# Four GNN layers in one kernel: layer 0's first layer norms in pairs, and the row sums of the adjacency matrix shared by VectorE and POOL

## The chip, the cores and the metric

The kernel runs on one core of a Trainium2 chip. The metric is the device time of one execution in microseconds (us). The core has five engines that work side by side and wait for each other through semaphores: TensorE (PE in the profile, with its weight loads as PEld), VectorE (DVE), ScalarE (ACT), GpSimd (POOL) and SyncE (SP), which here only issues DMA transfers. An engine runs its own instructions strictly in the order in which they were recorded.

## The reference

There are 4096 nodes with 64 features each, and one dense 4096 x 4096 float32 adjacency matrix `adj` (64 MiB), which all four layers use. Each layer computes `x = x + layer(relu(layernorm(x)), adj)`. Cut to what matters here:

```python
# layer 0                       h = adj @ h;  x += relu(h @ W.T + b)
# layer 1                       h = lorentz(h, W); q = lorentz(h, Wq); k = lorentz(h, Wk)
att = adj * sigmoid((2 + 2 * (qm @ k.T)) / att_scale + att_bias)
support = att @ h             # then each row is divided by its Lorentz norm
# layer 2
deg = jnp.maximum(adj.sum(axis=1, keepdims=True), 1e-08)
w = adj / deg
log_ij = _logmap(x[:, None, :], x[None, :, :], c)
agg = jnp.einsum('ij,ijc->ic', w, log_ij)
# layer 3                       ranks of the non-zero entries of each row, then w @ support
```

The row sums `deg` are needed in layer 2 alone. Since the matrix passes through the core in every layer anyway, the kernel makes them while it is there for layers 0 and 1.

## The kernel before, in words

**Tiling.** The 4096 rows are eight row blocks `ib` of 512 rows. For each block the transposed matrix comes in 16 groups `g`; a group is one tile `adj` of 128 partitions x 2 x 512 floats (512 KB), issued by `feed` on SP's queue, in a fixed order. Ten buffers hold such tiles in layers 0 and 1 (a pool of six and one of four). A buffer is free again when all readers of its tile are done (`used` counts them for the planner); SP's next issue into it waits for that.

**Layer 0.** `before0(ib)` makes the layer norm of 512 rows into `HA`: two reductions and two element-wise steps on VectorE, a square on ScalarE, and the power -0.5 on POOL (`power`, a tensor_tensor with `ALU.pow`). It is called once for each of the eight blocks. `l0_sums` adds each `adj` tile times `HA` into a PSUM accumulator `acc`; group `g` needs the rows of block `g // 2`, so already the first block of sums needs all eight layer norms. When the last group of a block is in, `after0` (ScalarE copies `acc` to `e`, PE multiplies by `W0T`, VectorE adds to `x`) and then `before1` (layer norm, two Lorentz linears, transposes to `qT` and `kT`) follow.

**Layer 1.** For each pair of tiles: `l1_atts` (PE, `mm<-qT,kT`), `l1_sigmoids` (ScalarE), `l1_weights` (VectorE, `sig<-sig,adj`), `l1_sums` (PE, `acc<-sig,HL`); after the last of a block `after1`, and `before2` for layer 2. Blocks 0 and 1 run together at first, with groups 14 and 15 kept for later, since these need the last block of `kT`.

**Row sums.** `degree_sums(layer, work)` adds tiles on VectorE into a buffer `dg` (128 x 2 x 512): the first by a copy, each further one by a tensor_tensor. Blocks 0 and 7 add all 16 tiles in layer 0; blocks 1 to 6 add 12 in layer 0 and the four of `LEFT` in layer 1. `after0` and `after1` add the two halves of `dg`, sum over partitions on PE (`tr<-ones_f,dg`), and write or add to `deg`.

**Order.** The instructions of all stages are recorded by generators that yield an engine and a due time. `in_turn` picks the one that can start first by the planner `Pace`, whose `cost` estimates each operation's duration; so a change of a cost or of a due time can shift the order on every engine, in the later layers too. The layer norms and what follows a block stand in a queue `tail`, of which the first two entries advance at a time. Tensors in `Pace.KEPT` (among them `HA`, `x` and `RT`) carry no due time for the planner, but the recorded waits between engines are real. `constants` issues the parameter loads on ScalarE's queue from 20 us of planned time, and at 36 us records `later_constants`: patterns that layers 1 to 3 need.

**Layers 2 and 3.** Layer 2 goes by tile pairs through a chain PE, ACT (`v<-mm`), POOL (`l2_clamps`, `v<-v`), ACT, DVE, PE. When a block is complete, `after2` and `before3` follow, with two POOL powers (`r_nn` and `ln_r`). Layer 3 does not use POOL for its tiles. Every instruction passes the recording helper `InOrder`, so the profile gives one line, L129, to nearly all.

The functions that the change touches:

Of the kernel before, what the change touches and what calls it, by code (L numbers as in the profile page):

```python
# [18 lines left out]
P = 128  # L19
# [5 lines left out]
CB = W // P  # L25
G = 2
NG = NC // G
LEFT = (3, 7, 11, 15)
EARLY = 12
BEHIND = NG - CB // G  # L30
LATE = BEHIND - CB // G
# [27 lines left out]
class Pace:  # L59
# [16 lines left out]
    def cost(self, engine, op, out, ins, rest, kw):  # L76
        n = per_partition(out)
        if engine == "PE":

            w, x = ins[0], ins[1]  # L80
            shape = [32 if k <= 32 else 64 if k <= 64 else 128 for k in (w.shape[0], per_partition(w))]
            change = 0.0 if shape == self.shape else 0.11
            self.shape = shape
            if op == "transpose":
                return change + 0.14
            share = 1 if n < 128 else min(128 * 128 // math.prod(shape), 4)
            passes = 4 if x.dtype == F32 else 1
            return change + max(passes * n / 2400 + 0.06, 0.27 if passes == 4 else 0.06) / share
        if engine == "ACT":
            if any(arg is AF.Sigmoid for arg in rest):  # L90
                n += n // 6
            return 0.18 + n / 1200 + (0.19 if "accum_out" in kw else 0.0)
        if engine == "POOL":
            return 1.65 if ALU.pow in kw.values() or n <= 8 else 0.25 + n / 300
        many = [ap for ap in ins if per_partition(ap) > 1]
        big = max([n] + [per_partition(ap) for ap in ins])
        psum = any(self.name(ap).split("_")[0] in ("mm", "acc", "tr") for ap in ins)
        return 0.12 + big / (1920 if len(many) <= 1 and not psum and op != "tensor_reduce" else 960)
# [38 lines left out]
def kernel(ctx: ExitStack, tc: tile.TileContext, a: dict, out: bass.AP):  # L137
# [111 lines left out]
    def later_constants():  # L249


        ACT.activation(es, scal[:, 0:3], AF.Exp)

        DVE.reciprocal(att_a, scal[:, 4:5])
        DVE.tensor_scalar(att_a, att_a, 2.0, None, ALU.mult)
        DVE.tensor_add(att_b, att_a, scal[:, 3:4])
        for t, one in [(t, 1.0) for t in rbs] + [(t, 0.25) for t in lbs]:
            POOL.memset(t, 0.0)
            for k in (1, 3):
                POOL.memset(t[:, :, k, 1:2], one)  # L260


        near_f = st["rows"].tile([P, P], F32, name="near_f", bufs=1)
        make_lower_triangular(nc, near_f, val=-STEP, diag=False)
        for q in range(4):
            b = slice(q * Q, (q + 1) * Q)
            DVE.tensor_copy(far[b, :], near_f[b, b])
        diag_f = st["rows"].tile([P, P], F32, name="diag_f", bufs=1)
        DVE.tensor_scalar(diag_f, ident, STEP * MAX_NEIGH, None, ALU.mult)
        DVE.tensor_add(near_f, near_f, diag_f)  # L270
        DVE.tensor_copy(near, near_f)


        DVE.memset(pick, 0.0)
        DVE.memset(spread, 0.0)
        for k in range(KH):
            DVE.memset(pick[:, k, k : k + 1], 1.0)
        for r in range(4):
            b = slice(r * Q, (r + 1) * Q)
            for h in range(2):  # L280
                to = spread[b, h, :, h * NC // 2 : (h + 1) * NC // 2]
                DVE.tensor_copy(
                    to.rearrange("p q (k r) -> p q k r", r=4)[:, :, :, r],
                    ident[b, r * Q : r * Q + KH].unsqueeze(1).to_broadcast([Q, 4, KH]),
                )

    def cs(ib):
        return slice(ib * CB, (ib + 1) * CB)

    def ws(ib):  # L290
        return slice(ib * W, (ib + 1) * W)
# [4 lines left out]
    def rt(name, shape, dtype=F32):  # L296
        return rows.tile(shape, dtype, tag=f"{name}_{slot['now']}", name=name, bufs=1)
# [38 lines left out]
    def bank():  # L336
        k = spare.pop(0)
        t = ps_tr.tile([P, W], F32, tag=f"tr{k}", name="tr", bufs=1)
        in_use.append((t, k))
        return t  # L340
# [78 lines left out]
            )  # L419


    def before0(ib, st):
        yield from layernorm_relu(ib, st["h0"][:, cs(ib), :])

    def before1(ib, st):
        h = rt("h", [P, CB, D])
# [121 lines left out]
    def after0(ib, acc, st):  # L548
        e = rows.tile([P, W], F32, tag="e", name="e")
        ACT.copy(e, acc)  # L550
        st["acc_free"][ib % 2] = pace.latest
        yield ON_V, lambda: st["dg_done"].get((0, ib))
        dg = st["dg"][0, ib]
        DVE.tensor_add(dg[:, 0, :], dg[:, 0, :], dg[:, 1, :])
        yield TURN

        ps = bank()
        v, n = ps[:, 0 : CB * D].rearrange("p (c k) -> p c k", k=D), CB * D
        for c in range(CB):
            b = slice(c * P, (c + 1) * P)  # L560
            PE.matmul(v[:, c, :], e[:, b], W0T, start=True, stop=True)
            PE.matmul(ps[:, n + c : n + c + 1], dg[:, 0, b], ones_f, start=True, stop=True)
        st["dg_free"][ib % 2] = pace.latest
        yield ON_V
        DVE.tensor_copy(deg[:, cs(ib), :], ps[:, n : n + CB].unsqueeze(2))
        s = rt("h", [P, CB, D])
        DVE.tensor_add(s, v, b0.to_broadcast([P, CB, D]))
        DVE.scalar_tensor_tensor(
            x[:, cs(ib), :], s, 0.0, x[:, cs(ib), :], ALU.max, ALU.add
        )  # L570
        yield ON_V

    def after1(ib, acc, st):
        e = rows.tile([P, W], F32, tag="e", name="e")
        ACT.copy(e, acc)
        st["acc_free"][ib % 2] = pace.latest
        yield ON_V, lambda: st["dg_done"].get((1, ib)) if (1, ib) in st["dg"] else 0.0
        dg = st["dg"].get((1, ib))
        if dg is not None:
            DVE.tensor_add(dg[:, 0, :], dg[:, 0, :], dg[:, 1, :])  # L580
        yield TURN
        ps = bank()
        v, n = ps[:, 0 : CB * D].rearrange("p (c k) -> p c k", k=D), CB * D
        for c in range(CB):
            b = slice(c * P, (c + 1) * P)
            PE.matmul(v[:, c, :], e[:, b], twice, start=True, stop=True)
            if dg is not None:
                PE.matmul(ps[:, n + c : n + c + 1], dg[:, 0, b], ones_f, start=True, stop=True)
        if dg is not None:
            st["dg_free"][ib % 2] = pace.latest  # L590
        yield ON_S
        s = rt("h", [P, CB, D])
        ACT.copy(s, v)
        sq = rt("r_sq", [P, CB, D])
        ACT.activation(sq, v, AF.Square)
        if dg is not None:
            new = rt("r_c", [P, CB, 1])
            ACT.copy(new, ps[:, n : n + CB].unsqueeze(2))
        yield ON_V
        if dg is not None:  # L600
            DVE.tensor_add(deg[:, cs(ib), :], deg[:, cs(ib), :], new)
        n = rt("r_n", [P, CB, 1])
        DVE.tensor_reduce(n, sq[:, :, 1:D], AX.X, ALU.add)
        DVE.tensor_sub(n, n, sq[:, :, 0:1])
# [106 lines left out]
    def latest(*times):  # L711
        return None if None in times else max(times)

    def in_turn(threads):
# [31 lines left out]

    st = {
        "h0": HA[:, :, 0:D],
        "dg": {}, "dg_done": {}, "acc_free": [0.0, 0.0], "dg_free": [0.0, 0.0],
    }  # L750
    rows_at = {}
    opened = {}
# [65 lines left out]


    def group(layer, ib, g):  # L820
        degree = (g in LEFT and 0 < ib < NB - 1) == (layer == 1)
        return {"layer": layer, "ib": ib, "g": g, "degree": degree, "left": 1 + degree, "at": 0.0}

# [25 lines left out]
            )  # L851
        return accs[k]

    def degree_sums(layer, work):

        dg = st["dg"]
        for d in work:
            if not d["degree"]:
                continue
            first = (layer, d["ib"]) not in dg  # L860
            yield "DVE", lambda: latest(
                arrival(d, 3.0), st["dg_free"][d["ib"] % 2] if first else 0.0
            )
            if first:
                t = w01.tile([P, G, W], F32, tag="dg", name="dg", bufs=2)
                dg[layer, d["ib"]] = t
                st["dg_free"][d["ib"] % 2] = None
                DVE.tensor_copy(t, d["adj"])
            else:
                t = dg[layer, d["ib"]]  # L870
                DVE.tensor_add(t, t, d["adj"])
            used(d)
            if d is [e for e in work if e["degree"] and e["ib"] == d["ib"]][-1]:
                st["dg_done"][layer, d["ib"]] = pace.latest

    for ib in range(NB):
        follow(with_mark(0, ib, before0(ib, st)))
        tail[-1]["at"] = 4.5 + 0.4 * ib

    def l0_sums():  # L880
        for d in l0:
# [10 lines left out]
    def constants():  # L892
        for k in range(len(loads) - 1):
            yield "ACT", lambda: 20.0 + 0.5 * k
            loads.pop(0)()
        loads[0]()
        yield "ACT", lambda: 36.0
        later_constants()
        loads.pop(0)

# [80 lines left out]

    def second_part():

        yield "ANY", lambda: latest(l1[-1].get("summed"), *st["dg_free"])
        early.close()
        adj_pools.pop()
        late["pool"] = ctx.enter_context(tc.tile_pool(name="late", bufs=1))
# [414 lines left out]
    def l3_sum():  # L1404
# [39 lines left out]
            (l2_coshs(), 0, once), (l2_weights2(), 1, lambda d: 2 if d["two"] else 1 if d["first"] else 0),  # L1444
        ),
        l2_clamps(), l2_gathers(), l3_weights(), l3_pass(), l3_counts(), l3_masks(),
        degree_sums(0, l0), degree_sums(1, l1), constants(),
    ])


# [43 lines left out]
```

## Time and profile before

| what | value |
|---|---|
| time, median of 3 runs | 1186.83 us (1185.45 to 1261.08) |
| profiled execution, its own time | 1186.61 us |
| span from first to last instruction in it | 1184.6 us |
| PE busy | 1078.5 us (91%) |
| DVE busy | 929.3 us (78%) |
| ACT busy | 783.1 us (66%) |
| POOL busy | 324.3 us (27%) |
| bytes moved by DMA | 271.76 MB |
| mean granted TensorE clock | 0.976 |

About 2.0 us of the profiled execution lie outside the span. Layer 0's last accumulator is copied out at 211.59 us, layer 1's last at 485.60 us, and layer 2's tile work ends near 960 us. In the view by stages each row gives the stretch, its length, the busy time of PE, PEld, DVE, ACT and POOL with the number of instructions, the granted TensorE clock, the busy share of the DMA engines and the rate in GB/s. In the timeline a row gives start, duration, engine, line, operation, tiles (`out<-in`), shapes, how many were merged, and in brackets the idle time of the engine before it and what ended it.

### The profile page before, as it was taken

To read this page: it belongs to the slowest core of one execution; us is meant where nothing else is said; L and a number is where in the kernel's file an instruction comes from. 1 tells how busy PE (TensorE), PEld (TensorE's weight loads), DVE (VectorE), ACT (ScalarE), POOL (GpSimd) and SP (SyncE) were. 2 spreads that over 40 slices of the span, in tenths; PEclk is the share of its full clock that TensorE was granted. 3 is DMA by queue.
4 is the path that set the end of the run, shared out by engine and by line. 5 is a ranking of instruction groups with operands and counts; after the bars stand their busy time and mean duration, and the time that the engine had idled before them with its cause. 6 is when DMAs were issued, how large, how long until landed. Compare 5 with 4: busy or idle time off the path is not lost.

```text
span 1184.6 us, 15638 instructions
## 1 busy us (share of the span) xinstructions
PE 1078.5 (91%) x5367; PEld 449.7 (38%) x5392; DVE 929.3 (78%) x1523; ACT 783.1 (66%) x1250; POOL 324.3 (27%) x172
## 2 busy tenths in 40 slices
PE   3899999999999999889989989999889789999997
PEld 1234444333333333244444444444344333333332
DVE  6888888869988988688888888898989985555550
ACT  1055456777767766789988778787876655555554
POOL 2222321102000010344454464464654420000000
PEclk9898999999999999899999999999998999999999
DMA  7899999865777765535434534444364389888830
GB/s 275 330 405 350 401 378 348 303 216 199 245 249 235 249 232 192 195 107 196 162 128 172 175 121 166 160 150 163 113 206 151 124 343 367 321 314 312 303 112 9
DMA packets 77191, 271.76 MB, mean 229 GB/s; under 512 B 10040, under 2 KB 11064, under 8 KB 77112
## 3 DMA queue, kind: packets, MB, share of 16 engines
q1 hardware_dynamic: 75456, 270.57, 63.7%
q8 instruction: 42, 0.69, 0.2%
q10 hardware_dynamic: 1656, 0.20, 0.1%
q14 instruction: 37, 0.30, 0.1%
HBM read 269.68 MB, written 1.05 MB: 229 GB/s over the span
## 4 chain that ended last, share of the span: by engine, by line
PE 49%; DVE 18%; ACT 11%; issue 10%; POOL 8%; DMA 3%; SPq 0%; ACTq 0%; POOLq 0%; DVEq 0%
PE acc L129 23%; PE mm L129 17%; PE tr L129 8%; DVE dg L129 5%; POOL v L129 4%; ACT wt L129 3%; DVE w L129 3%; ACT v L129 2%; DMA adj<-in_adjT_dram 2%; ACT t L129 2%; DVE t L129 2%; POOL lo_s L129 1%; DVE sig L129 1%; ACT sig L129 1%; POOL ln_r L129 1%
## 5 line engine op out<-in xcount | busy, mean ns | idle before, releaser
L129 PE MATMUL acc<-w,HA 128*65 128x256 f32 (+1 forms) x736 | 256.3, 485 | 13.0 <-DVE others L129 7.1
L129 POOL TENSOR_SCALAR v<-v 128x1024 f32<-128x1024 f32 x72 | 204.8, 2845 | 211.5 <-ACT v L129 205.4
L129 ACT ACTIVATE wt<-mm 128x1024 uint16<-128x1024 f32 x124 | 120.3, 1021 | 94.1 <-PE mm L129 94.1
L129 ACT ACTIVATE sig<-mm,att_b,att_a 128x1024 f32<-128x1024 f32 x128 | 148.3, 1202 | 40.9 <-PE mm L129 39.9
L129 DVE TENSOR_TENSOR sig<-sig,adj 128x1024 f32<-128x1024 f32 x128 | 152.5, 1221 | 25.2 <-ACT sig L129 25.0
L129 PE MATMUL acc<-adj,HA 128*64 128x512 f32 x512 | 128.4, 639 | 24.3 <-DVE HA L129 24.1
L129 DVE TENSOR_TENSOR dg<-dg,adj 128x1024 f32<-128x1024 f32 x114 | 139.2, 1221 | 2.2 <-DMA adj<-in_adjT_dram 0.6
L129 PEld LDWEIGHTS acc<-w,HA 128*65 128x65 f32 x736 | 98.1, 143 | 104.7 <-issue 56.6
L129 PE MATMUL mm<-qT,kT 64*128 64x512 f32 x512 | 129.5, 619 | 3.3 <-ACT sig L129 3.3
L129 PE MATMUL acc<-sig,HL 128*64 128x512 f32 x512 | 123.3, 604 | 1.6 <-DVE sig L129 1.5
L129 DVE SCALAR_TENSOR_TENSOR t<-mm,t 128x1024 f32<-128x1024 f32 x72 | 83.6, 1161 | 44.4 <-ACT t L129 43.9
L129 PE MATMUL acc<-wt,S 128*64 128x512 bf16 (+1 forms) x479 | 97.7, 387 | 3.5 <-issue 2.4
L129 PE MATMUL mm<-RT,LT 64*128 64x512 f32 (+1 forms) x288 | 79.7, 631 | 15.9 <-DVE t L129 15.2
L129 ACT ACTIVATE t<-t 128x1024 f32<-128x1024 f32 x72 | 72.6, 1008 | 31.9 <-DVE t L129 31.3
L129 ACT ACTIVATE v<-mm 128x1024 f32<-128x1024 f32 x72 | 69.8, 970 | 30.7 <-PE mm L129 30.6
L129 POOL TENSOR_TENSOR ln_r<-ln_v,minus_half 128x4 f32<-128x4 f32 x32 | 49.3, 1542 | 148.7 <-DVE ln_v L129 148.7
L129 DVE TENSOR_TENSOR w<-t,adj 128x1024 f32<-128x1024 f32 x72 | 84.0, 1167 | 1.5
L129 DVE SCALAR_TENSOR_TENSOR t<-t,v 128x1024 f32<-128x1024 f32 x72 | 83.7, 1163 | 1.8 <-ACT t L129 0.9
L129 ACT ACTIVATE v<-v,minus 128x1024 f32<-128x1024 f32 x72 | 78.4, 1089 | 7.8 <-POOL v L129 7.7
L129 DVE TENSOR_TENSOR w<-tr,adj 128x512 f32<-128x512 f32 x120 | 77.5, 681 | 1.1 <-PE tr L129 1.1
L129 PE MATMUL tr<-ident,t 128*128 128x128 f32 x480 | 66.1, 280 | 11.9 <-DVE t L129 8.2
L129 DVE TENSOR_SCALAR RT<-adj 128x1024 bf16<-128x1024 f32 x74 | 50.4, 698 | 33.3 <-PE mm L129 33.0
(208 smaller groups left out, 1395.6 us busy)
## 6 DMA issues: line engine op xcount, KB each, us to landing
adj<-in_adjT_dram SPq DMA_DIRECT2D x512, 512.0 KB, 4.8
x<-in_x_dram SPq DMA_DIRECT2D x4, 256.0 KB, 3.7
out_dram<-h SPq DMA_DIRECT2D x8, 128.0 KB, 2.8
b<-in_b_dram ACTq DMA_DIRECT2D x2, 32.0 KB
W<-in_W_dram ACTq DMA_DIRECT2D x3, 16.0 KB, 4.4
W0T<-in_W0T_dram ACTq DMA_DIRECT2D x2, 16.0 KB, 3.4
W1T<-in_W1T_dram ACTq DMA_DIRECT2D x1, 16.0 KB, 3.4
W1T<-in_b_dram ACTq DMA_DIRECT2D x1, 0.2 KB
```

The source lines that it names most:

```text
L129: done = self.tc.keep_in_program_order(getattr(self.engine, op)(*args, **kw))
```

## The change

Four things are edited.

1. `before0(k)` now makes the layer norm of two blocks (1024 rows) at once; it is called four times instead of eight. Its scratch lies in `HL` and `qT`, which layer 1 fills later.
2. `later_constants` is split. The three steps that layer 1 needs stay in `constants`; the patterns of POOL are due at 60 us, those of VectorE at 150 us, in five pieces.
3. The row sums: of the 16 groups of each block, VectorE adds the eight even ones in layer 0 into `dg`; POOL adds groups 3, 7, 11 and 15 in layer 0 and groups 1, 5, 9 and 13 in layer 1, straight into `RT[:, ws(ib)]` (`RT` is filled with something else by layer 2's `before2` later). VectorE adds the two halves of `dg` to the same place. The partition sum moves from `after0` to `after1`, for all eight blocks.
4. The planner's costs for POOL change: a power of n columns costs 0.5 + 0.25 n (was 1.65), other operations 0.25 + n/390 (was n/300), a memset 0.11 + n/1200.

```diff
-LEFT = (3, 7, 11, 15)
+POOL_0, POOL_1 = (3, 7, 11, 15,), (1, 5, 9, 13,)
+FRONT_0, FRONT_1 = (3, 7, 11, 15,), (1, 5, 9, 13,)
...
         if engine == "POOL":
-            return 1.65 if ALU.pow in kw.values() or n <= 8 else 0.25 + n / 300
+            if op == "memset":
+                return 0.11 + n / 1200
+            return 0.5 + 0.25 * n if ALU.pow in rest else 0.25 + n / 390
...
+        def patterns():
+            yield "POOL", lambda: 60.0
...
+        def weights_of_ranks():
+            yield "DVE", lambda: 150.0
...
-    def before0(ib, st):
-        yield from layernorm_relu(ib, st["h0"][:, cs(ib), :])
+    def before0(k, st):
+        c = slice(2 * k * CB, 2 * (k + 1) * CB)
+        xs, xc, to = x[:, c, :], st["HL"][:, c, :], st["h0"][:, c, :]
+        sq = st["qT"][:, 2 * k * W : (2 * k + 1) * W].rearrange("p (c d) -> p c d", d=D)
+        m, v, r = (rt(name, [P, 2 * CB, 1]) for name in ("lo_g", "lo_t", "lo_n"))
+        DVE.tensor_reduce(m, xs, AX.X, ALU.add)
+        DVE.scalar_tensor_tensor(xc, m.to_broadcast(xs.shape), -1.0 / D, xs, ALU.mult, ALU.add)
+        yield ON_S
+        ACT.activation(sq, xc, AF.Square)
+        yield ON_V
+        DVE.tensor_reduce(v, sq, AX.X, ALU.add)
+        DVE.tensor_scalar(v, v, 1.0 / D, LN_EPS, ALU.mult, ALU.add)
+        power(r, v, -0.5)
+        yield ON_V
+        DVE.scalar_tensor_tensor(to, xc, 0.0, r.to_broadcast(xs.shape), ALU.max, ALU.mult)
...
     def after0 (ib, acc, st):
-        yield ON_V, lambda: st["dg_done"].get((0, ib))
-        DVE.tensor_add(dg[:, 0, :], dg[:, 0, :], dg[:, 1, :])
-            PE.matmul(ps[:, n + c : n + c + 1], dg[:, 0, b], ones_f, start=True, stop=True)
-        DVE.tensor_copy(deg[:, cs(ib), :], ps[:, n : n + CB].unsqueeze(2))
+        v = yield from times(e, W0T, D, ON_V)
...
     def after1(ib, acc, st):
+        yield TURN, lambda: None if sums_left[ib] else 0.0
+            PE.matmul(
+                ps[:, n + c : n + c + 1], RT[:, (ib * CB + c) * P : (ib * CB + c + 1) * P], ones_f,
+                start=True, stop=True,
+            )
+        ACT.copy(deg[:, cs(ib), :], ps[:, n : n + CB].unsqueeze(2))
...
     def group(layer, ib, g):
-        degree = (g in LEFT and 0 < ib < NB - 1) == (layer == 1)
+        late = g in (POOL_1 if ib else FRONT_1)
+        by = "POOL" if late or g in (POOL_0 if ib else FRONT_0) else "DVE"
+        degree = by if late == (layer == 1) else None
...
+    def degree_sums():                      # VectorE's share, layer 0
+            for d in mine:
+                if d is mine[0]:
+                    DVE.tensor_copy(t, d["adj"])
+                else:
+                    DVE.tensor_add(t, t, d["adj"])
+            yield "DVE", lambda: opened.get(("sums", ib))
+            for c in range(G):
+                DVE.tensor_add(RT[:, ws(ib)], RT[:, ws(ib)], t[:, c, :])
+
+    def degree_sums_beside(work):           # POOL's share
+            to, ib = RT[:, ws(d["ib"])], d["ib"]
+            yield "POOL", lambda: arrival(d, 3.0)
+            if ("sums", ib) in opened:
+                POOL.tensor_tensor(to, to, d["adj"][:, 0, :], ALU.add)
+                yield "POOL", lambda: 0.0
+                POOL.tensor_tensor(to, to, d["adj"][:, 1, :], ALU.add)
             else:
+                POOL.tensor_tensor(to, d["adj"][:, 0, :], d["adj"][:, 1, :], ALU.add)
+                opened["sums", ib] = pace.latest
...
-    for ib in range(NB):
-        follow(with_mark(0, ib, before0(ib, st)))
-        tail[-1]["at"] = 4.5 + 0.4 * ib
+    for k in range(NB // 2):
+        follow(before0(k, st))
+        tail[-1]["at"] = 4.3 + 0.4 * k
```

## The prediction

> **What bounds the kernel now.** I read the view by stages first, then the timeline of the front, then the tile views of the operations that the change moves, last the chain of waits.
>
> ```profile
> 0.00:50.00 50.00, 25.88 (x86) 7.33 (x88) 39.15 (x86) 5.30 (x11) 13.21 (x36) 0.90 0.81 287
> 50.00:100.00 50.00, 46.61 (x236) 21.09 (x234) 43.20 (x68) 21.27 (x85) 11.53 (x6) 0.93 1.00 390
> 100.00:150.00 50.00, 47.22 (x258) 21.56 (x256) 41.45 (x68) 24.27 (x99) 14.36 (x7) 1.00 0.99 382
> 150.00:210.00 60.00, 58.50 (x304) 25.05 (x302) 52.11 (x79) 34.88 (x122) 11.89 (x7) 1.00 0.94 363
> 210.00:490.00 280.00, 270.23 (x1238) 99.00 (x1234) 232.43 (x449) 200.74 (x365) 32.98 (x20) 1.00 0.70 233
> 490.00:960.00 470.00, 425.26 (x1948) 199.75 (x1950) 409.89 (x593) 375.42 (x441) 236.03 (x93) 0.96 0.44 156
> 960.00:1185.00 225.00, 204.79 (x1306) 75.92 (x1328) 111.06 (x185) 121.25 (x131) 4.30 (x4) 1.00 0.71 260
> ```
>
> Layer 0 (to 210 us) is held by transfers: DMA share 0.94 to 1.00, PE next to full, VectorE 41 to 43 of 50 us. Layer 1 (to 490) is held by PE, 270 of 280 us, with DMA at 0.70. In layer 2 PE, DVE and ACT alternate. So a VectorE microsecond saved in layer 1 is worth little; in layer 0 what counts is the stream of tiles.
>
> Five-microsecond slices of the same view show up to 419 GB/s. At 417 a tile of 524,288 B takes 1.26 us. Against that rate the first 50 us owe 45 x 417 + 5 x 169 (first slice) less 50 x 287 = 5.3 MB, **12.6 us**; 50 to 210 owe 160 x 417 less 60.4 MB moved = 6.3 MB, **15.1 us**. The front's debt has its reason in the timeline:
>
> ```profile
> 33.05 1.01 POOL L129 TENSOR_TENSOR ln_r<-ln_v,minus_half 128x4 f32<-128x4 f32 x1 [2.11 <-DVE ln_v L129]
> ...
> 35.84 1.85 POOL L129 TENSOR_TENSOR ln_r<-ln_v,minus_half 128x4 f32<-128x4 f32 x1 [1.78 <-DVE ln_v L129]
> ...
> 37.45 1.83 DVE L129 CAST far<-near_f 32x32 bf16<-32x32 f32 x4 [0.18 <-issue]
> ...
> 40.59 1.05 DVE L129 CAST spread<-ident 32x16 bf16<-32x16 f32 x8
> 41.68 0.43 DVE L129 SCALAR_TENSOR_TENSOR HA<-ln_xc,ln_r 128x256 f32<-128x256 f32 x1
> ...
> 42.16 10.18 PE L129 MATMUL acc<-adj,HA 128*64 128x512 f32 x40 [3.42 <-DVE HA L129]
> ...
> 45.52 0.59 ACT L129 COPY e<-acc 128x512 f32<-128x512 f32 x1 [11.23 <-PE acc L129]
> ```
>
> The eighth layer norm reaches `HA` only at 41.68, behind 5 us of constants on VectorE; PE waits for it, no buffer comes free, the transfers pause. The first accumulator leaves at 45.52.
>
> **The change, term by term.**
>
> *Front.* With 1024 rows at once a reduction or step takes about 0.69 us (the 512-column rows: `dg<-dg` 0.686), a ScalarE square 0.6, the power of 8 columns 1.64 (`lo_s` with no neighbour). In the recorded order: reduce 4.36 to 5.05, centre to 5.8, square to 6.45, reduce and scale to 7.4, power to 9.1, next pair's two steps and reductions, `HA` of blocks 0 and 1 at about 11.1; the others at 14.7, 18.4 and 20.3. Now they come at 16.2 to 41.7. Tiles 5, 9 and 13, the first to need blocks 2, 4 and 6, land near 15, 20 and 25, so PE follows the arrivals and block 0 ends near 31 instead of 45.5. POOL begins its additions only after its four powers, about 19.4, which holds tiles 4 and 8; ten buffers cover that in part. I take 9 of the 12.6 us back: **-9** (bounds -12 and -4). ScalarE's parameter loads and SP's order are unchanged. The constants move to about 150 us on VectorE; there VectorE's freed time hides them. Without that cover they cost their 5 us.
>
> *VectorE and POOL in layer 0.* Now an inner block costs VectorE 0.69 + 11 x 1.22 + 0.69 + 0.16 = 15.0 us of sums and 5.3 of the rest, 20 of the 22 us that a block lasts. After: 0.69 + 7 x 1.22 + 2 x 0.69 = 10.6, with the rest 15.9. POOL gets 7 additions of 512 columns. No row has them; the nearest is `x<-x,b`, 256 columns, 0.727 us: doubled 1.45, or 1.35 with the slope of the `v<-v` rows (2.77 at 1024, 1.51 at 512). Above lies an addition that each time first waits for a whole `dg` step: 1.45 + 1.22 = 2.67. For these engines do block each other:
>
> ```profile
> L129 POOL TENSOR_TENSOR x<-x,b 128x256 f32<-128x256 f32 x8 | 6.4, 797 | 0.0
> L129 DVE TENSOR_TENSOR dg<-dg,adj x114: 1216/1220/1227, 11.2 to 446.5; 128x1024 f32<-128x1024 f32 x114
> 703.12 3.01 POOL L129 TENSOR_SCALAR v<-v 128x1024 f32<-128x1024 f32 x1
> 703.41 1.26 DVE L129 SCALAR_TENSOR_TENSOR hb<-ln_xc,ln_r 128x256 f32<-128x256 f32 x1
> 709.33 1.26 DVE L129 TENSOR_TENSOR hb<-hb,S 128x256 f32<-128x256 f32 x1
> ```
>
> A 256-column step of two SBUF tensors takes 0.42 us; beside POOL's `v<-v` it takes 1.26. The power of 4 columns takes 1.01 us alone, 1.85 when a `dg` step is under way (the two rows of the front above). I take half a `dg` step of waiting: 1.45 + 0.6 = 2.05 per addition, 14.4 a block; three powers add 1.6 on average, 5 us: 19 of 22 us, nearly full but not the bound. VectorE loses at most 0.84 per addition, 6 us: 15.9 + 6 = 22 at the worst, 18 likely.
>
> The Trainium skill, page "SBUF — State Buffer", section "Who interferes with whom", speaks against the change: a VectorE instruction with two SBUF inputs and a GpSimd one that reads SBUF exclude each other for the whole instruction. The trace agrees that they exclude each other, but the 0.42 us step behind a `v<-v` of 2.81 us ends after 1.36 us, so the hold seen is about 0.94 us. By the page's rule VectorE would lose 1.45 per addition, 10 us a block, and become layer 0's bound at 26 us: near 1200 us in all.
>
> PE loses eight column sums in layer 0: `tr<-W0T,e` and `tr<-ones_f,dg`, 16 records from 52.27 to 54.15, half of that 0.94 a block. The order shows another thing: when layer 0's last tile is summed, PE has done 6 pairs of `mm<-qT,kT` and 5 of `acc<-sig,HL` of layer 1, now 4 and 3. At 1.92 and 1.87 us a pair that is 7.6 us of layer 1 inside layer 0.
>
> New waits: VectorE's two additions into `RT` wait for POOL's last addition before them, up to 3 us a block; behind them stand the next block's `dg` steps, and for these SP's next tile. POOL's powers stand behind additions that wait for a tile's landing; for them wait `h`, `HL`, `qq` of `before1`, which has a block's time to spare except at the end. Of the 15.1 us debt I take **-4** back, from VectorE's relief (bounds -12, and +10 where POOL binds).
>
> *Layer 1.* -7.6 us done before. +0.94 x 2 for the column sums of blocks 0 and 7, less 0.94 in `after0` of block 7. But groups 14 and 15 need the last `kT`, now 43.3 us behind the last accumulator of layer 0 (211.59 to 254.88); PE then has 30.3 us of pairs and 7 of the rest before it, so it may idle up to 5.8 us there; I take 3. Sum **-4** (bounds -7 and +8, where POOL's 64 additions hold up the `sig` steps; VectorE has 0.69 + 3 x 1.22 + 0.69 + 0.16 = 5.2 us of 35 freed per block to hide them).
>
> *Layer 2.* The lower POOL cost puts `ln_r` behind the next `v<-v` at five block ends. There now, in the chain of waits (start, duration, what):
>
> ```profile
> 701.26 1.87 POOL ln_r L129
> 703.13 2.99 POOL v L129
> ```
>
> so the `v<-v` whose input is ready at 701.94 starts at 703.12, 1.18 us late. Five times: **-4** (bounds -6, and +5 for the shifted order at the start of layer 3, whose rows I can't price).
>
> Sum against the profiled execution's own time (span 1184.6 and 2.0 around it): 1186.6 - 9 - 4 - 4 - 4 = **1165.6 us**, say 1165. The median of the runs is 0.2 above that execution, which is nothing.
>
> **Rivals.** *Stream at its floor.* VectorE alone made the debt of 50 to 210 us; with it relieved tiles flow at 1.26 us: -12 -12 -4 -6, 1152. For it: VectorE at 83 to 90% with `dg` steps the last reader of most tiles. Against: between 90 and 100 us PE was the last, on transposes, at a granted clock of 0.54 to 0.78.
>
> *Given back.* The front is won, but tiles that POOL holds longer, and the chain to the last `kT`, return it: -9 +5 +0 +0, 1182. For it: POOL at 19 of 22 us, and PE nearly full in layer 0.
>
> *POOL binds layer 0* (the slower one). Each addition waits a full `dg` step, 2.67, and each power takes its blocked 1.92, 1.92 and 2.49: 7 x 2.67 + 6.3 = 25 us a block. From the first addition at 20 that puts layer 0's end at 222 and more instead of 211.6: +10, and +2 for layer 1: 1199. It decides from 2.2 us per addition on ((22 - 6.3)/7). Against: POOL reached the port between two back-to-back `dg` steps each time.
>
> **Numbers.** Forecast 0.46 (its own range 1156 to 1175), floor 0.26, given back 0.18, POOL binds 0.10. The four reach from 1146 (floor, with every bound of layer 2) to 1199; leaving out the upper end of POOL's case, and half of it by 1188, gives 1146 to 1188. Two per cent below 1186.83 is 1163.1, about what a measurement of this kernel can tell from no change: floor nearly all, and some 0.4 of the forecast's range, lie below it: faster 0.43. Slower by over 2% needs additions near 3 us: 0.05. The rest, 0.52, is within.
>
> **What would show it.** Right: PE's first `acc<-adj,HA` near 11 us, the first `e<-acc` near 31, DMA share of 0 to 50 us over 0.95; `RT<-RT,adj` on POOL of 1.4 to 2.1 us; layer 0's last `e<-acc` near 198 and layer 1's near 468; at five block ends `ln_r` behind `v<-v`. Wrong: additions over 2.2 us with POOL full from 20 to 200 us; `sig<-sig,adj` well over 1.22 with PE idle in layer 1; a first accumulator at 40; or layer 2 longer than now by more than 5 us.

## The result, and the profile after

The changed kernel takes **1234.93 us** (median of 4 runs, 1233.22 to 1243.12) against 1186.14 before on the same chip. One execution before, of 1261.08 us, fell into a slower state of the chip and is left out of the ratio, which is 1.0431, 95% interval 1.0403 to 1.0458. The kernel is slower by some 49 us; 1165 was forecast. The profiled execution has a span of 1231.5 us (before 1184.6).

The view by stages after, cut at 50, 100 and 150 us as before and then where the layers end here (columns as there: stretch, length, busy us of PE, PEld, DVE, ACT and POOL, granted clock, DMA share, GB/s):

```profile
0.00:50.00 50.00, 30.19 (x118) 9.15 (x120) 35.75 (x46) 6.87 (x11) 27.24 (x31) 0.93 0.86 315
50.00:100.00 50.00, 41.41 (x204) 15.85 (x202) 36.81 (x51) 22.89 (x87) 30.53 (x31) 1.00 0.95 365
100.00:150.00 50.00, 44.30 (x204) 17.92 (x200) 41.44 (x45) 24.05 (x86) 32.57 (x21) 0.90 0.83 304
150.00:235.00 85.00, 70.63 (x340) 27.37 (x342) 77.62 (x102) 38.37 (x135) 52.18 (x32) 0.98 0.88 319
235.00:529.00 294.00, 265.21 (x1190) 95.04 (x1186) 247.66 (x409) 194.78 (x357) 141.20 (x80) 0.99 0.65 217
529.00:997.00 468.00, 422.81 (x1936) 199.23 (x1937) 398.39 (x575) 371.18 (x436) 229.39 (x90) 0.96 0.43 152
997.00:1231.00 234.00, 210.81 (x1336) 78.10 (x1358) 116.63 (x204) 126.58 (x139) 7.83 (x6) 0.99 0.70 260
```

Layer 0 now lasts to 235 us instead of 212, and in its last 85 us no engine is full: PE 70.6, VectorE 77.6, POOL 52.2, transfers at 0.88. Layer 1 takes 294 us instead of 274, with PE idle for 29 of them.

The front came in part as it was said, as the timeline shows (start, duration, engine, line, operation, in brackets the idle time before it):

```profile
10.41 0.69 DVE L133 SCALAR_TENSOR_TENSOR HA<-HL,lo_n 128x512 f32<-128x512 f32 x1
...
11.15 10.61 PE L133 MATMUL acc<-adj,HA 128*64 128x512 f32 x40 [11.15 <-DVE HA L133]
...
19.64 1.75 DVE L133 SCALAR_TENSOR_TENSOR HA<-HL,lo_n 128x512 f32<-128x512 f32 x1 [0.39 <-POOL lo_n L133]
...
36.47 0.59 ACT L133 COPY e<-acc 128x512 f32<-128x512 f32 x1 [3.94 <-PE acc L133]
```

The last `HA` is there at 20 us instead of 42, and the first accumulator leaves at 36.5 instead of 45.5 (31 was expected, and a DMA share of over 0.95 in the first 50 us; it is 0.86). But that last `HA` step lasts 1.75 us where its fellows take 0.69: a POOL addition had begun 0.07 us before it. The groups of the page show the same on a large scale (count, then busy us and mean ns of one, then the idle time before):

```profile
L133 POOL TENSOR_TENSOR RT<-RT,adj 128x512 f32<-128x512 f32 x112 | 191.3, 1710 | 129.6 <-DMA adj<-in_adjT_dram 107.8
L133 DVE TENSOR_TENSOR sig<-sig,adj 128x1024 f32<-128x1024 f32 x128 | 185.5, 1479 | 26.1 <-ACT sig L133 25.4
L133 DVE TENSOR_TENSOR dg<-dg,adj 128x1024 f32<-128x1024 f32 x56 | 84.5, 1509 | 0.8
```

Before, `sig<-sig,adj` and `dg<-dg,adj` took 1.22 us without exception. The tile views give the spread (min/median/max in ns, first and last start):

```profile
L133 DVE TENSOR_TENSOR sig<-sig,adj x128: 1210/1224/2303, 199.4 to 520.9; 128x1024 f32<-128x1024 f32 x128
L133 DVE TENSOR_TENSOR dg<-dg,adj x56: 1210/1224/2291, 18.0 to 234.7; 128x1024 f32<-128x1024 f32 x56
L133 POOL TENSOR_TENSOR RT<-RT,adj x112: 1257/1556/2565, 20.9 to 499.6; 128x512 f32<-128x512 f32 x112
```

The median has not moved; some steps take 2.3 us, which is 1.22 and 1.06. I call the time by which a VectorE step exceeds the shortest step on the same tiles its **added time**. It sums to 47.9 us in layer 0 and 51.3 in layer 1 (before 2.8 and 1.4), for 120 POOL additions: 0.83 us each.

By stages, from the two traces: the first `e<-acc` 9.1 us earlier, the rest of layer 0 32.0 longer, layer 1 20.5 longer, from there to layer 3's first `e<-acc` 2.8 longer, the rest 0.6. Apart from rounding, this is the 46.9 us by which the spans differ.

### The profile page after: what moved, and what is told of

Read it like the earlier page. It is cut to its first block, busy times and chain, and to the rows that moved or that the text cites. A ratio compares the mean times of both kernels' runs of the same rounds, so it can differ in the third digit from the quotient of the medians.

```text
span 1231.5 us, 15553 instructions
## 1 busy us (share of the span) xinstructions
PE 1085.4 (88%) x5319; PEld 442.6 (36%) x5344; DVE 954.3 (77%) x1427; ACT 784.7 (64%) x1248; POOL 520.9 (42%) x288
## 4 chain that ended last, share of the span: by engine, by line
PE 40%; DVE 23%; issue 13%; ACT 12%; POOL 8%; DMA 4%; ACTq 0%; POOLq 0%; SPq 0%; DVEq 0%
PE acc L133 20%; PE mm L133 14%; PE tr L133 6%; DVE w L133 4%; DVE sig L133 4%; DMA adj<-in_adjT_dram 3%; POOL RT L133 3%; ACT v L133 3%; ACT wt L133 3%; ACT t L133 2%; DVE dg L133 2%; POOL lo_s L133 2%; DVE t L133 2%; ACT sig L133 1%; POOL ln_r L133 1%
## 5 line engine op out<-in xcount | busy, mean ns | idle before, releaser
L133 POOL TENSOR_TENSOR RT<-RT,adj 128x512 f32<-128x512 f32 x112 | 191.3, 1710 | 129.6 <-DMA adj<-in_adjT_dram 107.8
L133 DVE TENSOR_TENSOR sig<-sig,adj 128x1024 f32<-128x1024 f32 x128 | 185.5, 1479 | 26.1 <-ACT sig L133 25.4
L133 PE MATMUL mm<-qT,kT 64*128 64x512 f32 x512 | 132.3, 630 | 14.2 <-ACT sig L133 13.7
L133 PE MATMUL acc<-sig,HL 128*64 128x512 f32 x512 | 126.2, 609 | 8.6 <-DVE sig L133 8.0
L133 DVE TENSOR_TENSOR dg<-dg,adj 128x1024 f32<-128x1024 f32 x56 | 84.5, 1509 | 0.8
```

The source lines that it names most:

```text
L133: done = self.tc.keep_in_program_order(getattr(self.engine, op)(*args, **kw))
```

## The experiments

Two theories stood for the two large terms. P: a POOL addition shuts VectorE's steps with two SBUF inputs out. B: POOL holds the `adj` tiles and waits for landings, which slows the stream and its own powers. A third, O, blames the new order and the gather, that is the partition sum that moved to `after1`. This table has all runs but the bench (ratio to the kernel before on the same chip; us from the traces; "on" is from layer 1's last `e<-acc` to layer 3's first):

| run | ratio, 95% interval | layer 0's end | layer 1 | on | added time, layers 0 and 1 |
|---|---|---|---|---|---|
| before | 1 | 211.6 | 274.0 | 503.1 | 2.8, 1.4 |
| after | 1.0431 (1.0403-1.0458) | 234.6 | 294.5 | 506.0 | 47.9, 51.3 |
| e1 memsets | 0.9960 (0.9944-0.9975) | 203.1 | 272.6 | 507.0 | 2.3, 8.2 |
| e2 constant | 1.0657 (1.0631-1.0682) | 235.9 | 323.0 | 507.0 | 47.0, 60.9 |
| e3 VectorE | 1.0025 (1.0013-1.0037) | 208.0 | 276.7 | 505.5 | 2.3, 2.4 |
| e5 layer 0 only | 1.0351 (1.0319-1.0382) | 253.3 | 272.6 | 506.7 | 54.0, 2.8 |
| e6 layer 1 only | 1.0182 (1.0150-1.0214) | 210.5 | 291.2 | 506.5 | 8.8, 52.2 |
| e4 front | 0.9996 (0.9986-1.0006) | 210.3 | 275.7 | 503.5 | 1.6, 1.4 |
| e7 costs | 1.0027 (1.0008-1.0045) | 216.3 | 280.2 | 495.5 | 2.3, 2.8 |
| e8 front, costs | 1.0112 (1.0086-1.0138) | 206.0 | 292.5 | 502.9 | 2.7, 2.6 |
| e10 front, early loads | 0.9961 (0.9941-0.9982) | 203.3 | 278.3 | 502.7 | 2.0, 1.8 |
| e11 front, spread loads | 0.9995 (0.9978-1.0012) | 209.7 | 275.4 | 503.6 | 1.7, 1.7 |
| e12 early loads | 0.9999 (0.9988-1.0010) | 209.3 | 277.3 | 502.3 | 2.8, 1.7 |
| e13 front, norms first | 0.9949 (0.9931-0.9966) | 207.9 | 275.4 | 502.2 | 2.3, 2.1 |
| e14 e13, early loads | 0.9989 (0.9977-1.0000) | 212.9 | 275.4 | 500.2 | 2.4, 2.1 |
| e15 e14, shorter wait | 0.9995 (0.9983-1.0008) | 210.9 | 273.8 | 502.8 | 1.8, 1.8 |

### What POOL's additions cost

**POOL busy, but reading nothing.**

```diff
-                POOL.tensor_tensor(to, to, d["adj"][:, 0, :], ALU.add)
+                POOL.memset(to, 1.0)
+                POOL.memset(to, 1.0)
```

(the same for each addition, and 0.78 us in the planner's cost of such a memset)

> The changed kernel, with each POOL addition of 512 columns replaced by two memsets of the same columns of RT (about 0.5 us each), so POOL's share of the degree sums is left out; POOL's busy time and place in the order stay close, but POOL reads nothing from SBUF. Theory P (a POOL addition shuts VectorE's steps with two SBUF inputs out for its whole 1.26 us, 34.5 us on sig<-sig,adj, 16.7 us on dg<-dg,adj and some 20 us on layer 0's chain steps): sig<-sig,adj returns to a mean near 1.22 us, layer 1's blocks from 37.2 to about 34.5 us, and the time falls from 1235 to 1170-1182. Rival B (adj tiles held by POOL, landings waited for, powers queued behind additions): also 1170-1185 here, since POOL touches no adj tile; the next run tells B from P. Rival O (the gather in the block rows and the new order cost it): 1220-1235, with sig<-sig,adj near 1.22 all the same.

Measured: 1180.94 us. `sig<-sig,adj` is back at 1.22, though POOL is busy beside it; the group lines of this run:

```profile
L133 DVE TENSOR_TENSOR sig<-sig,adj 128x1024 f32<-128x1024 f32 x128 | 152.9, 1221 | 47.7 <-ACT sig L133 41.9
L133 POOL MEMSET RT<- 128x512 f32 x240 | 128.3, 536 | 29.9 <-DVE RT L133 18.8
```

The gather is still in it, and PE, VectorE and ScalarE carry out the same instructions in the same order as in the changed kernel, so O falls. B needs the next run.

**POOL reading, but no `adj` tile.**

```diff
-                POOL.tensor_tensor(to, to, d["adj"][:, 0, :], ALU.add)
+                POOL.tensor_tensor(to4, to4, ident.unsqueeze(1).to_broadcast([P, CB, P]), ALU.add)
```

(`to4` is `to` seen as 128x4x128; the same for each addition)

> The changed kernel, with POOL adding a constant 128x128 tile, repeated four times, to RT in place of the two halves of the adj tile: POOL's share of the degree sums is wrong, its reads and its time are kept, but it neither holds an adj tile nor waits for one to land. Theory P: VectorE's steps stay as slow as in the changed kernel (sig<-sig,adj near 1.48 us, dg<-dg,adj near 1.5), 1220-1235. Rival B: sig<-sig,adj may stay slow, but DMA runs ahead again and the time falls to 1175-1190. Rival O: 1220-1235, so O is told from P by the run with memsets.

Measured: 1264.08 us. Layer 0 ends at 235.9, as in the changed kernel, although POOL holds no tile and waits for none: B falls there. (From 60 us to layer 0's end SP waits 40.0 us for POOL in the changed kernel, and not at all here.) The size was missed: layer 1 is 28 us longer than even in the changed kernel. PE's waits in it come to 42.5 us instead of 24.4, and PE is busy 10.6 us longer, at a mean granted clock of 0.947 against 0.988. The timeline of one row chain shows where the additions fall now:

```profile
367.62 3.98 POOL L133 TENSOR_TENSOR RT<-RT,ident 128x512 f32<-128x512 f32 x3
367.81 1.12 DVE L133 TENSOR_TENSOR Mc<-Mc,r_c 128x4 f32<-128x4 f32 x1
...
369.06 1.22 DVE L133 TENSOR_SCALAR Fc<-deg 128x4 f32<-128x4 f32 x1
...
370.41 1.22 DVE L133 TENSOR_SCALAR r_m<-r_c 128x4 f32<-128x4 f32 x1
```

Without a landing to wait for, POOL's additions run back to back while `before2` goes through its small steps, and steps of 0.14 to 0.16 us (`Fc<-deg`, `r_m<-r_c` and `Mc<-Mc,r_c` in the changed kernel's same chain) last 1.1 to 1.2 in four or five of the layer's seven blocks. In the changed kernel the additions are spaced out by the landings (POOL waited 99.6 us for them in layer 1), and they hit `sig` steps more: 29.0 of the layer's 51.3 us of added time lie there, against 15.3 of 60.9 here. So the price depends on what an addition meets.

**The same sums, issued on VectorE.**

```diff
-            yield "POOL", lambda: arrival(d, 3.0)
+            yield "DVE", lambda: arrival(d, 3.0)
-                POOL.tensor_tensor(to, to, d["adj"][:, 0, :], ALU.add)
+                DVE.tensor_tensor(to, to, d["adj"][:, 0, :], ALU.add)
```

> The changed kernel, with the additions that POOL makes issued on VectorE instead: the same tiles, the same sums, the same gather in the block's rows, all correct. VectorE then carries 112 more additions of 128x512 (0.62-0.7 us each, some 75 us), which is what it had to add before. Theory P: sig<-sig,adj and dg<-dg,adj at 1.22 us, time 1170-1185. Rival B (adj tiles held too long by sums that come late): POOL's lateness goes, VectorE's additions come in the planner's order, 1175-1190. Rival O (gather and order): 1210-1235.

Measured: 1188.78 us, a little above P's range and inside B's, so this run does not part the two; the run with the constant does. Its group line for the moved additions:

```profile
L133 DVE TENSOR_TENSOR RT<-RT,adj 128x512 f32<-128x512 f32 x112 | 76.8, 688 | 1.7
```

VectorE does all of POOL's additions itself, 76.8 us more of them, and the kernel is 46 us faster for it. Nearly all that the change lost is in who adds; its other edits together come to +2.4 us here.

**One layer at a time.**

```diff
-POOL_0, POOL_1 = (3, 7, 11, 15,), (1, 5, 9, 13,)
-FRONT_0, FRONT_1 = (3, 7, 11, 15,), (1, 5, 9, 13,)
+POOL_0, POOL_1 = (3, 7, 11, 15,), ()          # e5; e6: (), (1, 5, 9, 13,)
+FRONT_0, FRONT_1 = (3, 7, 11, 15,), ()        # the same
```

(in the second, VectorE opens `RT` with the sum of the two halves of `dg`)

> The changed kernel with POOL's share of the degree sums in layer 0 alone (groups 3, 7, 11 and 15 of each block); the other twelve groups are VectorE's, all in layer 0, and nothing is added in layer 1. Theory P (each POOL addition shuts out VectorE's steps with two SBUF inputs, so the cost stands where the additions stand): layer 0's last e<-acc at 228-242 against 211.6 in the kernel before, layer 1 back to 272-276 us for the stage, time 1205-1220. Rival B (adj tiles held): much the same in layer 0, so this run tells it only by place. If the loss in layer 1 came from the gather, layer 1 stays at 290 and the time near 1230.

> The changed kernel with POOL's share in layer 1 alone (groups 1, 5, 9 and 13); the other twelve groups are VectorE's in layer 0, and POOL adds nothing there. Theory P: layer 0's last e<-acc at 204-212, HL<-hb,lo_s back from 1.48 to 0.42 us, layer 1 at 290-296 us against 274 before, time 1198-1212. If layer 0's loss were from the order of the front or the constants, it stays near 234 and the time near 1230.

Measured: 1228.71 and 1207.61 us. The loss stands where the additions stand: layer 1 takes 272.6 us without them and 291.2 with them, whatever layer 0 does. With them in layer 0 alone that layer ends at 253.3 and the time is 1228.71, both beyond what was expected (242 and 1220): VectorE has twelve tiles per block to add there instead of eight, and so more steps to be shut out (VectorE is busy 179.5 of the 193 us from 60 on).

**The price by itself.**

```diff
+    for of in ("none", "add", "max", "set", "pow"):
+        for kind in ("two", "one", "bank", "short"):
+            ...                                     # both engines start together
+            for k in range(8):                      # for kind "two"
+                DVE.tensor_add(t, t, other)
+            for k in range(8):                      # for of "add"
+                POOL.tensor_tensor(g[:, 0:W], g[:, 0:W], more, ALU.add)
```

> The kernel before, with a bench behind its end that adds time of its own: in turn every kind of VectorE step (1024 columns with two SBUF inputs; a copy of 1024; 512 columns from PSUM and SBUF; 256 columns with two SBUF inputs) runs eight times beside every kind of POOL work (none; additions of 512 columns; the max of 1024 columns as in v<-v; memsets of 512; powers of 4 columns). It prices the disputed term by itself. By the reading of the prediction (a hold of about 0.94 us whatever POOL does, at most 0.84 lost) a step of 1.22 beside additions takes at most 2.1 and one of 0.42 at most 1.3. By theory P (an addition shuts out two-input steps for its whole 1.26 us): up to 2.3 and 1.48, with POOL and VectorE taking turns, so 2.3-2.5 us for each pair. Copies of one input and steps from PSUM: no rise by the rows of layer 2 (t<-mm,t stays at 1.22 and 0.68). Memsets: no rise (dg<-dg,adj stayed at 1.22 beside them). The max: a rise of under 1 us in at most one step of three.

Measured, in us of one step in a steady row (VectorE's, then POOL's beside it):

| VectorE step | POOL idle | additions | max of 1024 | memsets | powers |
|---|---|---|---|---|---|
| 1024, two SBUF inputs | 1.22 | 2.17, 2.12 | 1.22 or 1.94, 3.15 | 1.22, 0.53 | 1.22, 1.18 |
| 256, two SBUF inputs | 0.42 | 1.37, 1.32 | 0.42 or 1.14, 2.77 | 0.42, 0.53 | 0.42, 1.01 |
| 1024, copy | 0.69 | 1.63, 1.59 | 0.69 or 1.40, 3.51 | 0.97, 0.95 | 0.69, 1.38 |
| 512, PSUM and SBUF | 0.69 | 0.69, 1.26 | 0.69, 2.77 | 0.69, 0.53 | 0.69, 1.01 |

The tile views of the first cell and, for contrast, the group lines of the PSUM cell and of a copy:

```profile
L129 DVE TENSOR_TENSOR two_add<-two_add,other x8: 2167/2168/2264, 1217.2 to 1232.7; 128x1024 f32<-128x1024 f32 x8
L129 POOL TENSOR_TENSOR pool_add_two<-pool_add_two,more x8: 1263/2124/2126, 1217.1 to 1231.6; 128x512 f32<-128x512 f32 x8
```

```profile
L129 DVE TENSOR_TENSOR bank_add<-bank_ps,other 128x512 f32<-128x512 f32 x8 | 5.5, 691 | 0.5 <-POOL tick L129 0.3
L129 DVE COPY one_add<-other 128x1024 f32<-128x1024 f32 x8 | 13.2, 1646 | 0.6 <-POOL tick L129 0.3
```

An addition costs the VectorE step beside it 0.94 us, or 1.04 where both start together (2.26 in the first pair), and beside the 1.22 us steps the addition itself loses 0.86. The hold is 0.94 to 1.04 of its 1.26 us, whether the step is long, short or a copy. The copies were expected not to rise, and did. A step that reads PSUM loses nothing.

### Where the front's gain went

**The front alone** (the change's first and second edit, with `degree_sums`, `after0` and `after1` as before).

> The kernel before with the first part of the change alone: layer 0's first rows two blocks at once, and the constants later and split; all degree sums stay on VectorE as before. The prediction's term for the front, -9 with bounds -12 and -4, and its rest of layer 0, kept apart from POOL: first e<-acc at 36-37 us against 45.5. If the gain is kept to the end: 1174-1178 against 1186. If it is given back (DMA stream at its limit in layer 0): 1184-1188, with layer 0's last e<-acc at 211 as before.

Measured: 1186.10 us. The first `e<-acc` comes at 40.1, not 36 to 37: VectorE takes five degree sums ahead of the first `HA`, which comes at 15.7 (10.4 in the changed kernel). That is the order which the planner's old costs give, not the old sums: with the same sums and the new costs (e8) the first `HA` comes at 10.1. The lead grows to 10 us at the fourth accumulator (102.9 against 112.9) and is 1.3 at layer 0's end.

**The planner's costs, alone and with the front** (the fourth edit alone; edits one, two and four).

> The kernel before with one edit: the planner's costs of POOL instructions, as the change has them (a power of four numbers 1.5 us in place of 1.65, a step of 1024 columns 2.88 in place of 3.66). It is to tell where the rest of the change's loss comes from: from layer 1's last e<-acc to layer 3's first, all kernels with the new costs and the gather took 505.5 to 507.1 us, the two with the old ones 503.1 and 503.6. If the costs do it: 505-507 in that stretch here and 1188-1190 in all; if the gather does it: 503 and 1185-1187. The prediction's term for layer 2 was -4 from these costs: then 499 and 1182.

> The kernel before with the front and the planner's costs, and the sums on VectorE as before: what is left of the change without sums on POOL. If the front is given back in layer 0's stream (the run with the front alone ended at 1186.1) and the costs are worth +3: 1188-1190. If the two gains of the prediction add up (-9 and -4): 1172-1176. If both come to nothing: 1185-1187.

Measured: 1188.89 and 1199.13 us. The costs alone are near the first expectation in all (+2.2 us), but not by its way: the stretch behind layer 1 is 7.6 us shorter, layers 0 and 1 are 10.9 longer. The costs alone also bring the last `HA` to 26.0 and the first `e<-acc` to 36.8, where the changed kernel has it, and the lead is lost again by layer 0's end (216.3). Together with the front the costs lose 12 us, which no theory said; layer 1 is 18.5 us longer, while VectorE's added time stays at 2.6. Of the 18.5 PE is busy 10.1 us longer, at a mean granted clock of 0.965 against 1.000. Only the order differs; which change of it does this stays open.

**The parameter loads.** In every kernel so far the stream runs at 178 to 228 GB/s in 20 to 35 us, also where `HA` is ready at 20. About that time (17.6 to 31.4 us before) ScalarE's queue issues 19 loads of 0.2 to 32 KB. In the recorded program all loads of both queues take eight completion semaphores in turn, and each waits until the load before it on the same semaphore has landed: before, from 12 to 46 us, SP waits 14.8 us for landings of `adj` and 3.1 for one of `scal`. That these waits are what slows the stream is argued; the runs show what moving the loads does.

```diff
-            yield "ACT", lambda: 20.0 + 0.5 * k
+            yield "ACT", lambda: 0.3 * k           # e10, e12; e11: 9.0 + 2.0 * k
```

(e10 and e11 on the front alone, e12 on the kernel before; in e11 the first block waits for the first fourteen loads only)

> The front alone, with one more edit: the 19 parameter loads on ScalarE's queue are due from 0 us of planned time in place of 20. Theory L: what holds the stream in 20-35 us (143 to 246 GB/s in every kernel so far, whatever HA does) are these loads: they share eight completion semaphores in turn with the adj loads, and each load waits for the one before it on the same semaphore. Then the rate in 20-35 us rises to 350 or more, the first e<-acc comes at 30-33, and the time falls to 1178-1182 against 1186 for the front alone. Rival: the stream was held by buffers that VectorE freed late, then 20-35 us stays under 260 GB/s and the time at 1184-1188. A loss is open too: loads at the start may delay x and the first tiles by 2-4 us.

> The front alone, with the parameter loads due one every 2 us from 9 us of planned time, in place of one every 0.5 us from 20; layer 0's first block then waits for the first fourteen only. Theory L: a load of a few KB behind adj tiles takes 5-6 us to land, but with one to two tiles between loads the stream stays above 330 GB/s in 20-35 us, the first e<-acc at 31-34, time 1178-1183. Rival (buffers): no change, 1184-1188.

> The kernel before, with the parameter loads due from 0 us as the only edit; the layer norms of layer 0 stay one block at a time. If the two causes in the front stand in parallel (the eighth HA at 41.7 holds PE whatever the stream does), nothing is won alone: first e<-acc at 43-46, time 1184-1188, and the front and the loads must be changed together. If the loads were the only cause: 1178-1182.

Measured: 1182.76, 1185.58 and 1186.75 us. The rows of 20 to 35 us, from the view by stages, of the front alone and then with early loads:

```profile
20.00:35.00 15.00, 12.59 (x54) 3.51 (x50) 14.46 (x15) 0.83 (x2) 3.58 (x2) 1.00 0.73 204
```

```profile
20.00:35.00 15.00, 15.00 (x66) 4.84 (x64) 13.90 (x18) 1.35 (x3) 4.12 (x2) 1.00 0.94 357
```

With early loads the stream is at 357 GB/s and PE busy for all 15 us, and 4 us are won, a little less than expected; the first `e<-acc` (35.0) is later than expected. Spread loads win nothing, and the rate of 20 to 35 us is 242 there, as the rival had it. On the kernel before early loads raise the rate to 382 there and win nothing, since `HA` holds PE until 41: two causes side by side.

**Norms first.**

```diff
             yield "DVE", lambda: latest(
-                arrival(d, 3.0), st["dg_free"][d["ib"] % 2] if first else 0.0
+                arrival(d, 3.0), st["dg_free"][d["ib"] % 2] if first else 0.0,
+                rows_at.get((0, NB - 1)),
             )
```

(e14 has the early loads too, e15 also 28 us in place of 36 for the end of the loads)

> The front alone (sums on VectorE, planner costs as before), with VectorE's degree sums due only when all layer norms of layer 0 are recorded; the parameter loads stay at 20 us. If the late HA hindered the front: HA at 10-20 us as in the changed kernel, first e<-acc at 36-37, time 1180-1183. If the stream of 20-35 us is the limit (theory L): HA at 10-20 us, but 20-35 us stays under 260 GB/s and the time at 1184-1187.

> As the run before it, with the parameter loads due from 0 us as well. Theory L: HA from 12-14 us, rate in 20-35 us over 350 GB/s, first e<-acc at 31-35, layer 0's last at 200-204, time 1177-1181. If PE is the limit from 20 us on, so that what is won at the front is PE's idle time before 20 us and no more: the same as with early loads alone, 1181-1184.

> As the run before it, with the end of the parameter loads set at 28 us of planned time in place of 36, since the last sum of the first block waits for it in the recorded order. If that order held the first accumulator at 35: first e<-acc at 29-32 and another 1-3 us off the time, 1175-1180. If it only changes what PE does first: no change against the run before, within 2 us.

Measured: 1180.69, 1185.31 and 1185.60 us. e13 has `HA` at 10.4 to 21.5 and wins 5.7 us, with the first `e<-acc` at 39.0 (36 to 37 was expected) and although its stream is slower in 20 to 35 us than that of the front alone:

```profile
20.00:35.00 15.00, 7.24 (x21) 1.72 (x23) 13.10 (x15) 0.20 (x1) 1.49 (x1) 0.66 0.51 178
```

VectorE's sums now start at 22 us, and SP waits 17.4 us for them (14 to 42 us). So the loads are not the only limit, as I had taken them to be: VectorE, which makes the norms and frees the tiles, is another. In e14 and e15 the squares of the later norms stand behind the early loads on ScalarE's queue, the last two `HA` come at 25.8 and 28.0 in e14 (25.6 and 27.8 in e15), and 20 to 35 us stay at 166 and 169 GB/s although the loads are early. Neither expectation of e14 came; of e15's the second did, no change against e14. **Of the versions with all sums made e13 has the lowest ratio to the kernel before, 0.9949 (0.9931 to 0.9966).** e10's 0.9961 (0.9941 to 0.9982) is not told apart from it. Neither has POOL's additions.

## Why the prediction was wrong

**Front, -9 (bounds -12 and -4).** In the changed kernel the first accumulator did come 9.1 us earlier, and PE's first sum at 11.15. But the planner's costs alone bring that accumulator 8.8 us earlier (e7), so the pairs of norms did not need to be the reason. As a gain that lasts to the end the front is worth 0 on the old sums (e4), outside the bounds, and 5.7 with VectorE's order mended (e13), inside them. What failed is the reason given for the debt: "the eighth layer norm" was one of three things that held the front, beside the parameter loads (e10) and VectorE's sums (e13).

**VectorE and POOL in layer 0, -4 (bounds -12 and +10).** Measured +32, of it +26.6 by POOL's additions (against e3). This is the step that failed. The price of a collision was near enough: "at most 0.84 per addition" against 0.80 on the average in layer 0 (47.9 us over 60) and 0.94 in the bench, which is also the hold that the prediction itself read from layer 2. From it I worked out "15.9 + 6 = 22 at the worst, 18 likely" for a block of 22 us. The six came in full, 47.9 / 8 = 6.0 a block; there was no reason to take a third of them. And I asked only whether VectorE's time fits a block. It did: between layer 0's first and last `e<-acc` VectorE is busy 142 of 166 us before, 150 of 171 in e3, and 164 of 198 after, so it was not full. What failed is the sentence that `h`, `HL` and `qq` of `before1` have "a block's time to spare". PE carries out the transposes of that row chain in order, between its sums, and waits for each of these three (60 to 230 us after):

```profile
PE tr L133 <- DVE HL L133: 10.4, 6, 3.5
PE tr L133 <- DVE h L133: 6.3, 5, 2.1
PE tr L133 <- ACT qq L133: 6.1, 5, 1.9
```

Before, these were 3.8, 2.5 and 1.1 us (60 to 215 us). The sum closes against e1, which has the same order of instructions: between the first and last `e<-acc` the changed kernel takes 30.8 us more; PE's waits are 29.5 us against 6.1 (27.2 against 4.8 of them at transposes), and PE is busy 7.5 us longer, at a granted clock of 0.96 against 1.00. Why the clock is lower no run shows. The waits are not for POOL's powers: VectorE's `HL`, `h` and `qq` wait 15.0 us for these, and 14.6 in e1. Each VectorE step stands in a queue in order, `dg` steps before the `HL`, `qq` and `h` of `before1`, and a delay of one is a delay of all behind it. Of the 45.6 us that VectorE's added time grows from e3 to the changed kernel, 26.6 lengthen layer 0; how much of it each delayed step carries stays open.

**Layer 1, -4 (bounds -7 and +8).** Measured +20.5, of it +17.8 by POOL's additions (against e3). Here the step that failed is "5.2 us of 35 freed per block to hide them". VectorE was busy for 83% of the layer before and 84% after, so it had the room; but `sig<-sig,adj` lies between ScalarE's `sig` and PE's `acc<-sig,HL`, and a step that is 1.06 us late on that path is not made good by idle time elsewhere. The waits in layer 1 (235 to 529 us) show the path (us in total, times, longest):

```profile
PEld acc L133 <- DVE sig L133: 33.0, 41, 2.6
PE mm L133 <- ACT sig L133: 13.0, 15, 2.1
PE acc L133 <- DVE sig L133: 7.5, 9, 1.7
```

Before, the first of these was 12.2 us in 19 waits. Against e1 the layer is 21.9 us longer: PE's own waits are 24.4 us against 8.6, and PE is busy 5.8 us longer, at a granted clock of 0.988 against 1.000. The term itself came at most in part: two pairs more are done before layer 0's last sum, as forecast, but without POOL's additions the layer takes 272.6 us (e1) or 276.7 (e3) against 274.0, so -1.4 or +2.7.

**Layer 2, -4.** The mechanism came: five `ln_r` start behind a `v<-v` and take 1.04 us instead of 1.87. The layer's last `e<-acc` is 2.9 us nearer to layer 1's, but layer 3's first then comes 5.7 later, and 4.5 later with the costs alone (e7): the shifted order that the prediction could not price. The term was +2.8; the bounds held it.

**POOL.** Additions took 1.71 us on the average (2.05 was taken), 1.26 without a neighbour (1.45 was taken), and POOL was busy 110 of 175 us in layer 0. So the slower rival, "POOL binds layer 0", had the direction right but not the mechanism: POOL was not full; the steps that it delays on VectorE cost the time.

**The reach.** Its lower end, 1146, takes layer 2's -6 twice, since the 1152 of the floor already has it; the four lower bounds add up to 1149.6.

**The rule that I weighed.** The Trainium skill, page "SBUF — State Buffer", section "Who interferes with whom", says that a VectorE step with two SBUF inputs contends with a GpSimd instruction that reads SBUF, and not with one that only writes it. The runs agree on both: 1.22 us beside memsets, 2.17 beside additions. By its exclusion "for the whole instruction" I had 1200 us, the right side; the bench has 0.94 to 1.04 of 1.26 us for an addition and 0.72 of 2.77 for a max, so there the measurement decides. That sum was near 1200 us because it made VectorE layer 0's bound, and VectorE was busy 164 of 198 us. My mistake was not between 0.94 and 1.26 but in what lies behind a delayed step.

## What to carry to other kernels

When work moves to an engine that shares a resource, price what the move does to every instruction of the other engine on a path with no slack, not only whether the busy time fits: here 76.8 us of additions taken from VectorE (what they cost it in e3) came back as 94.5 us of added time, in worse places. A collision's price depends on what it hits, and additions that nothing spaces out hit the row chains. A lull in the stream can have several causes side by side; until each is removed, removing one shows little.

## What was not expected of the hardware

- A VectorE copy of 1024 float32 with one SBUF input is shut out like a two-input step: 0.69 us alone, 1.63 beside POOL's additions, and 0.97 beside its memsets, which themselves rise from 0.53 to 0.95.
- A step with one operand in PSUM is not touched: 0.69 us beside everything that POOL did.
- POOL's max of 1024 columns blocks VectorE's two-input steps once per instruction in the bench, for 0.72 us of its 2.77 (0.82 where both start together); powers of 4 columns never block a step there for more than 0.04, and are themselves delayed by up to 0.53.
